# A decoder layer on one core: scores and projections two steps ahead until attention step 52 instead of 42

## The chip, the core and the metric

The kernel runs on one core of a Trainium2 chip. The metric is the time of one execution on the device in microseconds, as the median of several runs. The core has a matrix engine (TensorE, "PE" in the profile, with its weight loads as "PEld"), VectorE ("DVE"), ScalarE ("ACT"), GpSimd ("POOL") and SyncE ("SP"), which here only issues DMAs.

## What is computed

One decoder layer with pre-normalisation on x of shape 8 x 128 x 512, float32. Cut to what matters:

```python
# causal self-attention: 32 query heads, 8 key/value heads, head size 128
h = layernorm(x)
q, k, v = h @ w_q, h @ w_k, h @ w_v
probs = softmax(where(causal, q @ k.T * 128 ** -0.5, -inf))
x = x + (probs @ v) @ w_o
# attention over a context of the same shape
h = layernorm(x)
s = softmax(ctx @ h.T * 128 ** -0.5, axis=1)
x = x + s @ ctx
# gated feed-forward, three weight matrices packed in 4 bits
h = layernorm(x)
Wg, Wu, Wd = dequant(gate), dequant(up), dequant(down)
x = x + (silu(h @ Wg) * (h @ Wu)) @ Wd
```

The reference's attention over the context is `_L0_xattn_ref`, its 4-bit weights are those of `_L0_ffn_ref`.

## The kernel before

Every product is made from a high and a low 16-bit half of each operand, as three matmuls (high x high, high x low, low x high; `mm3`, lines 164 to 166). So each value that leaves the matrix engine is cast on ScalarE into its high half (line 118, in `split`) and subtracted on VectorE or GpSimd into its low half (line 121).

Self-attention is cut by key/value head into 8 groups `g` of four query heads, and by batch into two halves of four entries. A *unit* is one group with one half of the batch, a *step* is one group with one batch entry. There are 16 units of 4 steps, so 64 steps, numbered by `i`. The last four units are in another order than the rest: group 6 first half, group 7 first half, group 6 second half, group 7 second half (line 1050). Steps 40 to 43 are group 5 first half, 44 to 47 group 5 second half, 48 to 51 group 6 first half, 52 to 55 group 7 first half.

A step has four parts, each a function:

- `att_s` (line 587): the scores of one step, 12 matmuls into a bank of PSUM `ps_sc` (two banks, tag "s"); mask and row minimum on VectorE (line 608), exponentials on ScalarE (line 565), division by the sum on GpSimd (lines 575 and 622), the split into 16-bit halves `pb` on ScalarE and GpSimd, and a transposing DMA from `pb` to `pt`, issued on SP (line 636). The tile `s` has three buffers, `pb` two, `pt` three.
- `proj_piece` (line 1111, through `proj_parts`, line 1097): a quarter of the projections of one unit. Piece `j` of a unit makes one query head (`ps_q`, 12 matmuls of 512 columns); piece 0 also makes the unit's keys (`ps_k`), and pieces 1 and 2 of an even group make two batch entries of values each (`ps_v`), which are copied by two DMAs on SP (line 551). All of them share two banks of PSUM, tag "j". A piece's number is four times its unit plus `j`.
- `att_v` (line 639): probabilities times values, `ps_at`, five matmuls from line 645 on, then the cast `ah` (ScalarE) and the rest `al` (VectorE).
- `att_o` (line 653): those times the output weights, `ps_o`, 12 matmuls, added into `xr` on VectorE (line 662).

In `step(i)` the output product of step i-1 and the value product of step i come last, and before them the scores and the projection piece of a later step: one step ahead at the start, two steps ahead in the middle, one step ahead again afterwards. Two constants on line 1365, `SOON` and `BACK`, say when. At step `SOON` both the scores for one step and for two steps ahead are issued; at step `BACK` none, and neither a projection piece. From step `TAIL` = 53 on, `tail_step` (line 1335) takes over. It is one step ahead at first (scores two ahead from step 56 on) and mixes in the attention over the context. From step 53 on, the order on the matrix engine (until step 59) and on GpSimd is held to the order of the program. Elsewhere the order in which each engine gets its instructions is worked out when the kernel is built, from the program's order, the dependencies and estimated durations; it may pull later work forward where that is ready earlier. Once built, the order is fixed.

Between the steps other work is placed by step number. Weights of later groups are loaded into single buffers (`rawq`, `rawo`, `rawv`), their squares summed on ScalarE (`sumsq`, line 262, into `junk`) for a scale (lines 285 to 314), scaled on GpSimd (line 355) and split. The 4-bit weights of the feed-forward are unpacked on VectorE (lines 807 and 811) in steps 8 to 42. The context entries are loaded, summed and split in steps 43 to 53 (`c_load`, `c_prep`). The load of group 7's query weight is placed at step 40, and needs the buffer that group 6's last query weight leaves. The squares and the multiplies of this background work are held behind the exponentials and the multiplies of a given step, `pace["exp"]` and `pace["mul"]`; line 1400 picks that step.

Of the kernel before, what the change touches and what calls it, by code (L numbers as in the profile page):

```python
# [53 lines left out]
def tile_decoder(  # L54
# [1307 lines left out]
        for f in tail_x.pop((i, 1), ()):  # L1362
            f()

    SOON, BACK = 14, 42

    def step(i):
        g, b = steps[i]
# [118 lines left out]
```

## Time and profile before

| | us |
|---|---|
| median of three runs | 656.67 |
| lowest and highest of them | 656.52 to 656.84 |
| the profiled execution | 655.96 |
| its span, first to last instruction | 654.2 |

The granted clock of the matrix engine was 0.998 of full speed. The DMAs moved 69.34 MB, a mean of 106 GB/s. In the page's rows a group of instructions has a line of the kernel, an engine, an operation, what it writes and reads, a count, its busy time, the mean duration of one in nanoseconds, and the idle time of its engine before it with what ended most of that. These are the groups of the four parts of a step:

| part | group | count | mean ns |
|---|---|---|---|
| `att_s` | exponentials, ACT line 565 | 256 | 365 |
| `att_s` | mask and minimum, DVE line 608 | 256 | 310 |
| `att_s` | split of `pb`, ACT line 118 | 128 | 349 |
| `proj_piece` | cast `qh`, ACT line 118 | 64 | 571 |
| `proj_piece` | subtraction `ql`, DVE line 121 | 64 | 688 |
| `att_v` | cast `ah`, ACT line 118 | 64 | 582 |
| `att_v` | subtraction `al`, DVE line 121 | 64 | 683 |
| `att_o` | addition into `xr`, DVE line 662 | 64 | 747 |

Matmuls are pipelined: one of 512 columns is listed with some 378 ns but the next starts 216 ns after it. A stretch of the span can be asked for with the busy time of each engine in it; a timeline lists single instructions, with the idle time before one and what released it in square brackets.

### The profile page before, as it was taken

To read this page: it belongs to the slowest core of one execution; us is meant where nothing else is said; L and a number is where in the kernel's file an instruction comes from. 1 tells how busy PE (TensorE), PEld (TensorE's weight loads), DVE (VectorE), ACT (ScalarE), POOL (GpSimd) and SP (SyncE) were. 2 spreads that over 40 slices of the span, in tenths; PEclk is the share of its full clock that TensorE was granted. 3 is DMA by queue.
4 is the path that set the end of the run, shared out by engine and by line. 5 is a ranking of instruction groups with operands and counts; after the bars stand their busy time and mean duration, and the time that the engine had idled before them with its cause. 6 is when DMAs were issued, how large, how long until landed. Compare 5 with 4: busy or idle time off the path is not lost.

```text
span 654.2 us, 12431 instructions
## 1 busy us (share of the span) xinstructions
PE 629.8 (96%) x3992; PEld 342.3 (52%) x3992; DVE 465.6 (71%) x1475; ACT 439.3 (67%) x1238; POOL 380.8 (58%) x586
## 2 busy tenths in 40 slices
PE   8789999999999999999999999999999989999996
PEld 6455545565655555565555465556544434445443
DVE  6846676665767866576777555767776768988986
ACT  5687677465667675566667576866566478867674
POOL 7757477563747883475489395734577247612521
PEclk9999999999999999999999999999999999999999
DMA  9287254943763756355636414343544242102002
GB/s 316 48 171 170 75 72 122 229 105 79 190 164 88 187 137 160 95 168 127 151 94 167 143 41 122 66 92 74 89 67 68 39 93 50 31 19 65 1 1 64
DMA packets 117773, 69.34 MB, mean 106 GB/s; under 512 B 84190, under 2 KB 100593, under 8 KB 117708
## 3 DMA queue, kind: packets, MB, share of 16 engines
q1 hardware_dynamic: 117708, 68.55, 44.0%
q8 instruction: 31, 0.51, 0.3%
q14 instruction: 34, 0.28, 0.2%
HBM read 42.12 MB, written 2.20 MB: 68 GB/s over the span
## 4 chain that ended last, share of the span: by engine, by line
PE 73%; DVE 8%; DMA 6%; ACT 6%; POOL 4%; issue 2%; SPq 1%; DVEq 0%; ACTq 0%; POOLq 0%
PE ps_o L166 7%; PE ps_o L164 7%; PE ps_o L165 7%; PE ps_q L164 7%; PE ps_q L165 7%; PE ps_q L166 7%; PE ps_c L1181 6%; PE ps_c L1182 6%; DMA rawq<-in_L_attn_w_q_dram 3%; DMA pt<-pb 2%; PE ps_v L164 2%; PE ps_v L166 2%; PE ps_v L165 2%; PE ps_k L165 2%; PE ps_k L166 2%
## 5 line engine op out<-in xcount | busy, mean ns | idle before, releaser
L565 ACT ACTIVATE s<-s,negm 128x64 f32<-128x64 f32 (+1 forms) x256 | 93.1, 365 | 51.5 <-DVE negm L608 50.8
L164 PE MATMUL ps_q<-hT,wqh 128*128 128x512 f16 (+1 forms) x260 | 97.7, 376 | 1.6 <-DVE ql L121 1.6
L164 PE MATMUL ps_o<-woh,ah 128*128 128x512 f16 x256 | 97.0, 379 | 1.2 <-ACT ah L118 1.2
L166 PE MATMUL ps_o<-woh,al 128*128 128x512 f16 x256 | 96.9, 379 | 1.1 <-DVE al L121 1.1
L166 PE MATMUL ps_q<-hT,wql 128*128 128x512 f16 (+1 forms) x260 | 97.7, 376 | 0.0
L165 PE MATMUL ps_q<-hT,wqh 128*128 128x512 f16 (+1 forms) x260 | 97.7, 376 | 0.0
L165 PE MATMUL ps_o<-wol,ah 128*128 128x512 f16 x256 | 97.0, 379 | 0.0
L121 POOL TENSOR_TENSOR pb<-s,pb 128x256 f16<-128x256 f32 (+1 forms) x128 | 72.6, 582 | 16.2 <-ACT pb L118 14.3
L662 DVE SCALAR_TENSOR_TENSOR xr<-ps_o,unsc,xr 128x512 f32<-128x512 f32 x64 | 47.8, 747 | 41.3 <-PE ps_o L166 34.4
L575 POOL TENSOR_SCALAR rec<-rec 128x4 f32<-128x4 f32 x64 | 14.2, 222 | 108.1 <-DVE rec L573 87.5
L121 DVE TENSOR_TENSOR ql<-ps_q,qh 128x512 f16<-128x512 f32 x64 | 44.0, 688 | 40.3 <-ACT qh L118 40.2
L608 DVE CUSTOM_DVE_ANT_0 s<-ps_sc,mask,soft 128x64 f32<-128x64 f32 (+1 forms) x256 | 67.1, 310 | 4.0 <-PE ps_sc L166 1.9
L622 POOL TENSOR_TENSOR s<-s,rec 128x128 f32<-128x128 f32 (+1 forms) x128 | 63.6, 518 | 4.8
L118 ACT CAST pb<-s 128x256 f16<-128x256 f32 (+1 forms) x128 | 42.8, 349 | 28.1 <-POOL s L622 24.7
L118 ACT CAST ah<-ps_at 128x512 f16<-128x512 f32 x64 | 37.2, 582 | 21.9 <-PE ps_at L166 15.9
L565 ACT ACTIVATION_READ_ACCUMULATOR s<-s,negm 128x1 f32 x256 | 48.0, 188 | 0.0
L121 DVE TENSOR_TENSOR al<-ps_at,ah 128x512 f16<-128x512 f32 x64 | 43.7, 683 | 3.4 <-ACT ah L118 2.9
L1194 DVE TENSOR_SCALAR ps_c<-ps_c,rTg 128x512 f32<-128x512 f32 (+1 forms) x56 | 40.7, 750 | 7.0 <-PE ps_c L1182 6.4
L1192 ACT ACTIVATE ps_c<-ps_c,rTu 128x512 f32<-128x512 f32 (+1 forms) x57 | 36.2, 659 | 11.4 <-PE ps_c L1182 9.3
L118 ACT CAST qh<-ps_q 128x512 f16<-128x512 f32 x64 | 36.6, 571 | 10.6 <-PE ps_q L166 9.6
L166 PE MATMUL ps_sc<-k,ql 128*128 128x128 f16 (+1 forms) x256 | 42.6, 206 | 0.5 <-DVE ql L121 0.5
L165 PE MATMUL ps_sc<-k,qh 128*128 128x128 f16 (+1 forms) x256 | 41.5, 206 | 0.0
(244 smaller groups left out, 1698.3 us busy)
## 6 DMA issues: line engine op xcount, KB each, us to landing
rawq<-in_L_attn_w_q_dram SPq DMA_DIRECT2D x8, 1024.0 KB, 5.8
rawo<-in_L_attn_w_o_dram SPq DMA_DIRECT2D x8, 1024.0 KB, 6.1
zi<-zd SPq DMA_DIRECT2D x26, 256.0 KB, 4.1
vd<-v SPq DMA_DIRECT2D x64, 64.0 KB, 2.4
qr<-_L_ffn_down_qweight_dram SPq DMA_DIRECT2D x10, 256.0 KB, 5.8
xr<-in_x_dram SPq DMA_DIRECT2D x8, 256.0 KB, 8.2
rawk<-in_L_attn_w_k_dram SPq DMA_DIRECT2D x8, 256.0 KB, 5.7
rawv<-in_L_attn_w_v_dram SPq DMA_DIRECT2D x4, 512.0 KB
```

The costliest lines, as they stand in the source:

```text
L118: a = nc.scalar.copy(hi, src)
L121: b = (lo_eng or nc.vector).tensor_tensor(lo, src, hi, ALU.subtract)
L164: nc.tensor.matmul(ps, lh, rh, start=start and i == 0, stop=False)
L165: nc.tensor.matmul(ps, lh, rl, start=False, stop=False)
L166: nc.tensor.matmul(ps, ll, rh, start=False, stop=stop and i == n - 1)
L565: exp = nc.scalar.activation(v, v, AF.Exp, bias=negm[:, j : j + 1], scale=-1.0, accum_out=sums[:, j : j + 1],)
L608: nc.vector.tensor_tensor_reduce(view, flat(ps, cols[j]), masks[j // 2], soft_t[g][:, j % 2 : j % 2 + 1], BIG, ALU.add, ALU.min, negm,)
L622: mul = nc.gpsimd.tensor_tensor(v, v, rec[:, 2 * k : 2 * k + 2].unsqueeze(2).to_broadcast([P, 2, (k + 1) * HQ]), ALU.mult,)
L662: return nc.vector.scalar_tensor_tensor(xr[b], ps, unsc_t[g], xr[b], ALU.mult, ALU.add)
L1181: nc.tensor.matmul(ps, lh, rh, start=r == 0, stop=False, skip_group_check=r > 0)
L1182: nc.tensor.matmul(ps, lh, rl, start=False, stop=True, skip_group_check=r > 0)
L1194: nc.vector.tensor_scalar(ps, ps, sc, None, ALU.mult)
```

## The change

`BACK` goes from 42 to 52. Step 42 now issues the scores of step 44 and projection piece 48, and so on; steps 42 to 51 are two ahead, and step 52 is the one that issues neither. From step 53 on the program is the same. Line 1400 uses `BACK` as well, so that background work placed in steps 42 to 51 is held behind the exponentials and multiplies of step i+1 instead of step i.

```diff
-    SOON, BACK = 14, 42
+    SOON, BACK = 14, 52
 
     def step(i):
         g, b = steps[i]
```

## The prediction

> **What bounds the kernel now.** I read the page first, for the engine that sets the pace, then the table of stretches, for where that engine stops, then the timelines of the one stretch where the change starts. The page's first part:
>
> ```profile
> PE 629.8 (96%) x3992; PEld 342.3 (52%) x3992; DVE 465.6 (71%) x1475; ACT 439.3 (67%) x1238; POOL 380.8 (58%) x586
> ```
>
> TensorE (PE) is busy 96% of the 654.2 us. Its 512-column matmuls start 0.22 us apart wherever nothing waits (365.37, 365.59, 365.81 in the timeline), so in such stretches only less matmul work could help, and the change takes none away. What can be won or lost is idle time of PE. The stretches from attention step 41 to the end of attention show where that is (columns: stretch, its length, then busy time of PE, weight load, VectorE (DVE), ScalarE (ACT), GpSimd (POOL), granted clock, DMA):
>
> ```profile
> core 0: us, PE busy (x) PEld busy (x) DVE busy (x) ACT busy (x) POOL busy (x), PEclk, DMA share, GB/s
> 340.00:360.00 20.00, 20.00 (x137) 10.83 (x135) 16.34 (x54) 14.29 (x46) 18.29 (x27) 1.00 0.59 142
> 360.00:380.00 20.00, 17.69 (x122) 9.75 (x121) 11.22 (x46) 12.63 (x41) 9.31 (x16) 1.00 0.43 126
> 380.00:400.00 20.00, 20.00 (x130) 11.64 (x128) 9.45 (x31) 12.26 (x38) 18.48 (x27) 1.00 0.26 55
> 400.00:420.00 20.00, 20.00 (x139) 10.68 (x138) 15.04 (x77) 16.59 (x53) 10.40 (x18) 1.00 0.35 102
> 420.00:440.00 20.00, 20.00 (x131) 11.03 (x130) 12.74 (x54) 13.40 (x47) 9.91 (x16) 1.00 0.49 96
> 440.00:460.00 20.00, 20.00 (x159) 12.62 (x157) 14.73 (x58) 12.28 (x36) 9.71 (x18) 1.00 0.29 60
> 460.00:500.00 40.00, 37.52 (x266) 19.87 (x264) 28.03 (x112) 22.91 (x77) 26.80 (x44) 1.00 0.48 78
> ```
>
> Value products (line 645) of step 42 start at 361.03 and those of step 53 at 451.98. So the ten steps that the change re-orders, 42 to 51, lie in 360 to 440, and PE idles there in one place only: 20 - 17.69 = 2.31 us between 360 and 380, which is where the kernel drops from two steps ahead to one. The four waits of PE that make it up:
>
> ```profile
> 368.79 0.39 PE L164 MATMUL ps_o<-woh,ah 128*128 128x512 f16 x1 [0.57 <-ACT ah L118]
> 370.11 0.39 PE L166 MATMUL ps_o<-woh,al 128*128 128x512 f16 x1 [0.47 <-DVE al L121]
> ...
> 377.99 0.28 PE L645 MATMUL ps_at<-pt,vd 128*128 128x256 f16 x1 [0.63 <-DMA pt<-pb]
> 379.63 0.39 PE L164 MATMUL ps_o<-woh,ah 128*128 128x512 f16 x1 [0.64 <-ACT ah L118]
> ```
>
> The sum is 0.57 + 0.47 + 0.63 + 0.64 = 2.31. Counted by matmul starts against the usual spacing it is 2.97 (0.74 + 0.63 + 0.80 + 0.80), because the profile lets a matmul last longer than the next one waits. Two of the four wait for `ah`, the casts of attention results of steps 42 and 43. Why the first was late, from ACT's timeline:
>
> ```profile
> 360.63 0.40 ACT L118 CAST pb<-s 128x256 f16<-128x256 f32 x1 [0.27 <-POOL s L622]
> 365.60 0.63 ACT L262 ACTIVATE junk<-rawq 128x512 bf16<-128x512 f32 x1 [4.57 <-DMA rawq<-in_L_attn_w_q_dram]
> ...
> 368.17 0.56 ACT L118 CAST ah<-ps_at 128x512 f16<-128x512 f32 x1
> ...
> 369.25 0.34 ACT L565 ACTIVATE s<-s,negm 128x64 f32<-128x64 f32 x1
> ...
> 370.91 0.57 ACT L118 CAST k<-ps_k 128x512 f16<-128x512 f32 x1
> ```
>
> ACT stands 4.57 us on the sum of squares of the last query weight, whose load was issued at 359.74 and took 5.84 us. Behind it wait `ah` of step 42 (its matmuls were done at 363.90, it began at 368.17), the exponentials of step 44 and the evacuation of the key projection. The exponentials in turn hold up the probabilities `pt` of step 44, the third wait. VectorE stands behind the same load (3.5 us before its line 285).
>
> **The change part by part.** *The work moved.* Before, steps 43 to 52 issue scores for steps 44 to 53 and projection pieces 48 to 57; after, steps 42 to 51 do. No instruction is added or taken away. Moved one step up are 10 x 12 score matmuls (0.67 us a step, 452.55 to 453.22), 10 query pieces and 3 key pieces of 12 matmuls at 0.216 us (13 x 2.6 = 33.7 us) and 6 value pieces (12 x 0.109 = 1.3 us each, 7.8 us): 48 us of PE work, the same on both sides, so 0. The same for what hangs on it: 40 exponentials of 0.365 us, 40 masked reductions of 0.31, 10 + 3 casts of 0.57 with their subtractions of 0.69, 6 value evacuations, the POOL multiplies and splits.
>
> *Queues.* On SP go 10 probability transposes (1.2 us of queue each) and 12 value copies (0.6 each). A transpose of step i+2 now waits for its softmax one step earlier in the program, and context loads, weight loads and value copies queue behind it; SP already stands 29.5 us (12.6 + 11.9 + 3.1 + 1.9 in its waits by releaser) on such transposes between 380 and 460 with PE never idle there, so 0, and up to one `pt` wait (0.63 us) if that cover is gone. POOL and ACT meet the softmax ahead of `ah` instead of behind it. Priced at 0, because the same order has run in 340 to 360 at 20.00 of 20; without that cover one `ah` wait, 0.64 us.
>
> *Weights.* Projections move up by about one step, some 8 us, but their weights do not. The last group's four low parts are ready at 378.55, 379.66, 388.72 and 394.40 and its matmuls begin at 401.35, 407.59, 413.35 and 417.02: at least 22 us of slack, of which 8 go. 0. Value tiles (8 buffers) come free at least one step before they are needed, as in the earlier groups. 0. The pacing on line 1400 names the exponentials of one step later for steps 42 to 51; these too are issued a step earlier, so background work keeps its place. 0.
>
> *The gain at step 42.* Step 42 issued nothing but its output and value products; now scores of 44 and the key and query pieces of 48 come first. These 5.9 us had been pulled forward anyhow (they run from 359.07 to 368.1), so what is new as cover is the next step's: scores of 45 and query piece 49, 0.67 + 2.6 = 3.3 us, against 1.04 us of idle before 370.2; for the pair at 378 it is the softmax of step 44 that gets a place ahead of `ah`. Bounds: 0, if both projection banks are still full when PE gets there (the key cast at 370.91 frees one), and 2.31 to 2.97, if all four waits close. I take 2.31: moving the cast and the exponentials ahead of `ah` in the program is just what opens both banks.
>
> [...]
>
> *The step without scores and projections moves to 52,* right before the order written out by hand begins. There output products of step 51 follow the value products of 51 with little between them. Cover: value products of 52 (0.55 us) and, pulled forward, scores of 54 and query piece 58 (0.67 + 2.6), 3.8 us in all. Need: the shortest distance from value to output products in the trace is 2.1 us where PE did not idle (step 55: 468.38 to 470.47). Cost 0; 2.97 if a wait as at step 42 is met there, the nearest row.
>
> *Sum.* The profiled execution took 655.96 us, 1.8 of it outside the span. 654.2 - 2.31 + 0 = 651.9 of span, 653.65 with what is outside. The profiled execution lies 0.71 below the median of 656.67, so against the median: **654.4 us**.
>
> **The rivals.** *A, the hole is only moved, and grows (slower).* ACT's wait for the load stays ahead of everything, so 42 keeps its 2.97 us; at 52 the hand-written order lets PE pull nothing past a late `ah`, and a second 2.97 is paid. 656.67 + 2.97 = 659.6. For it: ACT also waits for context loads near there (2.24 us at 428.71). Against: PE idles 0 us from 380 to 460. It decides if `ah` of step 51 comes more than 3.8 us after its value products.
>
> *B, nothing to be seen.* The gap at 42 stays or moves whole, nothing else: 656.7. For it: scores and projections were pulled forward already, so the written order may matter little. Against: two banks then filled, which is what stopped PE.
>
> *C, the order of the rest shifts.* ACT and DVE are not held to the written order late in attention, and PE idles 2.48 us in 460 to 500 and 3.05 in 500 to 540. A shift by half of these 5.5 us each way: 653.9 or 659.4. For it: small waits of 0.3 to 1.1 us there hang on softmax and transposes. Against: from step 53 the issue order is the same in both kernels.
>
> **How the numbers follow.** What a measurement of this kernel tells from no change is about 0.2%, 1.3 us. Forecast (1.3 to 3.5 us saved): 0.44. A: 0.24. B: 0.19. C: 0.13, of it 0.03 on the fast and 0.10 on the slow side. Faster 0.44 + 0.03 = 0.47, same 0.19, slower 0.24 + 0.10 = 0.34. The forecast's own range is 653.2 to 655.4. The whole range reaches down to 652.6, where 2.97 and a little of C's gain fall together, and up to 660.0, past A by a small `ah` wait; about 0.2 is left outside.
>
> **What would show it.** Right: PE busy 20.0 of 20 in the stretch around the last query weight's load, exponentials of step 44 ahead of that weight's squares on ACT, and no new idle of PE between the value products of 51 and the output products of 52. Wrong: an `ah` wait of PE still at step 42, or one at 51 or 52 (A); idle of PE after 460 differing by more than 1.3 us (C). The forecast falls altogether if the wait for weights shows up as PE waiting on `wqh` or `wql`.

## The result, and the profile after

The changed kernel took 658.56 us (median of 22 runs, 656.68 to 660.38) against 656.47 for the kernel before, run beside it. The ratio is 1.0025, 95% interval 1.0015 to 1.0035. That is the ratio of the means and stands for some 1.6 us; the medians lie 2.1 us apart. So the kernel became slower, where 2.3 us faster was forecast. A second set of runs gave 1.0016 (1.0006 to 1.0026). The kernel before measured against itself gave 1.0001 (0.999 to 1.0011).

The execution profiled first took 657.65 us, its span 655.9. Its page again shows PE at 96%:

```profile
PE 631.5 (96%) x3992; PEld 343.2 (52%) x3992; DVE 468.6 (71%) x1475; ACT 440.4 (67%) x1238; POOL 380.2 (58%) x586
```

The same stretches as before the change (stretch, length, then busy time of PE, PEld, DVE, ACT, POOL, granted clock, DMA):

```profile
340.00:360.00 20.00, 20.00 (x137) 10.96 (x136) 15.89 (x54) 14.74 (x48) 18.12 (x27) 1.00 0.59 141
360.00:380.00 20.00, 17.72 (x120) 9.92 (x119) 11.33 (x40) 11.70 (x39) 7.45 (x15) 1.00 0.43 129
380.00:400.00 20.00, 20.00 (x138) 11.66 (x137) 11.99 (x47) 14.63 (x45) 19.34 (x28) 1.00 0.27 57
400.00:420.00 20.00, 19.69 (x132) 10.40 (x131) 11.22 (x55) 14.54 (x48) 8.55 (x17) 1.00 0.29 87
420.00:440.00 20.00, 20.00 (x129) 10.87 (x127) 14.95 (x62) 14.86 (x44) 14.34 (x22) 1.00 0.44 97
440.00:460.00 20.00, 19.43 (x137) 11.61 (x136) 14.45 (x59) 11.54 (x35) 6.96 (x14) 1.00 0.33 73
```

The idle time in 360 to 380 stayed (2.28 us instead of 2.31), and two new places joined it: 0.31 us in 400 to 420, 0.57 in 440 to 460. The rows of PE in its timeline that waited:

```profile
372.32 0.27 PE L164 MATMUL ps_v<-wvh,hT 128*128 128x256 f16 x1 [0.48 <-DVE ql L121]
...
374.35 0.17 PE L289 MATMUL ps_n<-sb,ones 128*128 128x4 bf16 x1 [0.89 <-DVE sb L285]
...
376.29 0.18 PE L289 MATMUL ps_n<-sb,ones 128*128 128x1 bf16 x1 [0.91 <-DVE al L121]
...
414.41 0.39 PE L164 MATMUL ps_o<-woh,ah 128*128 128x512 f16 x1 [0.21 <-ACT ah L118]
...
443.14 0.27 PE L645 MATMUL ps_at<-pt,vd 128*128 128x256 f16 x1 [0.57 <-DVE r L298]
```

All three places have the same thing in ACT's timeline, a sum of squares (line 262) that stands waiting for a load, with the cast `ah` of attention results behind it:

```profile
369.43 0.63 ACT L262 ACTIVATE junk<-rawq 128x512 bf16<-128x512 f32 x1 [3.06 <-DMA rawq<-in_L_attn_w_q_dram]
...
370.35 0.62 ACT L262 ACTIVATE junk<-rawq 128x512 bf16<-128x512 f32 x1
...
371.44 1.05 ACT L262 ACTIVATE junk<-rawo 128x1024 bf16<-128x1024 f32 x1
...
372.62 0.63 ACT L262 ACTIVATE junk<-rawq 128x512 bf16<-128x512 f32 x1
...
373.37 0.63 ACT L262 ACTIVATE junk<-rawq 128x512 bf16<-128x512 f32 x1
...
374.00 0.57 ACT L118 CAST ah<-ps_at 128x512 f16<-128x512 f32 x1
...
410.43 1.06 ACT L262 ACTIVATE junk<-rawo 128x1024 bf16<-128x1024 f32 x1 [2.30 <-DMA rawo<-in_L_attn_w_o_dram]
...
413.79 0.57 ACT L118 CAST ah<-ps_at 128x512 f16<-128x512 f32 x1
...
441.46 0.63 ACT L262 ACTIVATE junk<-c 128x512 bf16<-128x512 f32 x1 [1.22 <-DMA c<-in_ctx_dram]
442.09 0.57 ACT L118 CAST ah<-ps_at 128x512 f16<-128x512 f32 x1
```

They are group 7's query weights, its output weights and a context entry. (The sum over `rawo` at 371.44 is group 6's.) At the query weights the wait for the load is only the first part. When the load had landed, ACT worked for another 4.57 us (369.43 to 374.00) on what stood ahead of `ah`, all four query sums among it. Before the change only two of the four stood ahead, and `ah` began 2.57 us after the load (365.60 to 368.17).

To compare runs without the scatter of the start, I measure between marks: the first value-product matmul (line 645) of a step in the timeline. From step 40 to 53 lie the re-ordered steps; the idle time is PE's, summed over that stretch.

| kernel, profile | start to 40 | 40 to 53 | PE idle in it | 53 to 63 | 63 to the end |
|---|---|---|---|---|---|
| before, first | 349.70 | 102.28 | 2.31 | 77.75 | 124.46 |
| before, second | 351.49 | 102.30 | 2.15 | 77.74 | 124.48 |
| after, first | 350.38 | 103.29 | 3.16 | 77.74 | 124.47 |
| after, second | 350.61 | 104.15 | 4.03 | 77.73 | 124.48 |

The change acts in steps 40 to 53 alone, by +1.0 and +1.9 us. What follows is equal to a few hundredths, and what comes before scatters by 2 us whatever the kernel.

### The profile page after: what moved, and what is told of

Same layout as the page of the kernel before. It is cut to its first block, busy times and chain, and to the rows that moved or that the text cites. A ratio compares the mean times of both kernels' runs of the same rounds, so it can differ in the third digit from the quotient of the medians.

```text
span 655.9 us, 12430 instructions
## 1 busy us (share of the span) xinstructions
PE 631.5 (96%) x3992; PEld 343.2 (52%) x3992; DVE 468.6 (71%) x1475; ACT 440.4 (67%) x1238; POOL 380.2 (58%) x586
## 4 chain that ended last, share of the span: by engine, by line
PE 60%; POOL 12%; DVE 8%; DMA 7%; ACT 6%; issue 5%; SPq 1%; DVEq 0%; POOLq 0%; ACTq 0%
PE ps_c L1181 6%; PE ps_c L1182 6%; PE ps_o L166 6%; PE ps_o L164 6%; PE ps_o L165 6%; PE ps_q L166 5%; PE ps_q L164 5%; PE ps_q L165 5%; DMA pt<-pb 3%; POOL pb L121 2%; DMA rawq<-in_L_attn_w_q_dram 2%; POOL s L622 2%; POOL wql L121 2%; POOL wol L121 2%; DVE ps_c L1194 2%
## 5 line engine op out<-in xcount | busy, mean ns | idle before, releaser
L121 POOL TENSOR_TENSOR pb<-s,pb 128x256 f16<-128x256 f32 (+1 forms) x128 | 71.1, 571 | 19.8 <-ACT pb L118 18.0
L166 PE MATMUL ps_sc<-k,ql 128*128 128x64 f16 (+1 forms) x256 | 43.1, 207 | 0.5 <-DVE ql L121 0.5
```

What stands on the lines that cost most here:

```text
L121: b = (lo_eng or nc.vector).tensor_tensor(lo, src, hi, ALU.subtract)
L166: nc.tensor.matmul(ps, ll, rh, start=False, stop=stop and i == n - 1)
```

## The experiments

Theories: *P*, the pacing on line 1400 makes the load of group 7's query weights late; *O*, the new order of scores, projections and products costs by itself; later *L*, ACT meets the sums over late loads in front of the casts, whatever the order, and *H*, the step that issues no scores or projections leaves PE without cover. All ratios are to the kernel before, run beside it.

**Pacing and order apart.** Four kernels. Step 42's pacing undone in the changed kernel:

```diff
-paces[steps[i + (SOON < i < min(BACK, len(steps) - 1))]]
+paces[steps[i + (SOON < i < BACK and i != 42)]]
```

> The change with one thing undone: background work of step 42 alone is held behind the multiplies and exponentials of step 42, as before the change, not behind those of step 43. Theory P (pacing): in the changed kernel group 6's last query weight is finished 2.3 us later against the rest (362.70 instead of 359.35, of which 0.7 came in with the start), so group 7's load starts later and PE meets the wait for it. Then this kernel issues that load some 2 to 3 us earlier, PE idles less than 1.5 us in the 20 us around it instead of 2.28, and the time is 655.0 to 656.5, ratio to before 0.997 to 1.000. Theory O (order): scores and projections ahead of the output products cost by themselves. Then the time stays near 658, ratio 1.002 or more, with idle of PE after 400 as in the changed kernel (0.31 and 0.57 us).

The pacing of all ten steps undone:

```diff
-paces[steps[i + (SOON < i < min(BACK, len(steps) - 1))]]
+paces[steps[i + (SOON < i < 42)]]
```

> The change of order alone: pacing of steps 42 to 51 stays as before the change (background work behind step i, not i+1). Theory P: like the run with step 42 alone, ratio 0.997 to 1.000, because step 42 is the only step at which the pacing moves against the issue of the softmax by a whole step. Theory O: ratio 1.002 or more.

Pacing alone, with `BACK` at 42:

```diff
-paces[steps[i + (SOON < i < min(BACK, len(steps) - 1))]]
+paces[steps[i + (SOON < i < 52)]]
```

> The pacing alone: order of scores and projections as before the change, background work of steps 42 to 51 held behind step i+1. Theory P: the load of group 7's query weight starts later, the time goes up by 1 to 3 us, ratio 1.0015 to 1.005. Theory O: no change, ratio 0.999 to 1.001.

The pacing of step 42 alone, with `BACK` at 42:

```diff
-paces[steps[i + (SOON < i < min(BACK, len(steps) - 1))]]
+paces[steps[i + (SOON < i < 43)]]
```

> The pacing of step 42 alone, order as before the change. Theory P: as the run with the pacing alone, ratio 1.0015 to 1.005, since only this step holds the weight that the load waits for. Theory O: ratio 0.999 to 1.001.

| run | ratio (95%) | 40 to 53 | PE idle | query load issued after step 40's mark |
|---|---|---|---|---|
| step 42 paced as before | 1.0010 (0.9998 to 1.0022) | 103.76 | 3.75 | 9.66 |
| all paced as before | 1.0089 (1.0073 to 1.0104) | 109.02 | 5.74 | 9.71 |
| pacing alone | 0.9997 (0.9987 to 1.0007) | 103.03 | 2.60 | 12.37 |
| pacing of step 42 alone | 1.0039 (1.0022 to 1.0055) | 105.06 | 4.31 | 12.36 |

The load's issue obeys theory P exactly: about 9.7 us after the mark with step 42 paced as before (10.04 in the kernel before), 12.4 without (12.36 in the changed kernel). The times do not obey it: undoing all the pacing made the kernel much slower, and pacing alone changed nothing. Theory O had these two right (1.002 or more, and no change). But it too expected no change from the pacing of step 42 alone, which cost 2.6 us with the order untouched, and the first run, at 1.0010, lies outside the ranges of both. So these four runs decide for neither. The first shows why (stretches as above):

```profile
360.00:380.00 20.00, 19.57 (x136) 11.11 (x135) 11.32 (x45) 12.49 (x40) 8.34 (x16) 1.00 0.47 123
380.00:400.00 20.00, 19.31 (x126) 10.90 (x125) 10.06 (x39) 14.24 (x46) 19.06 (x28) 1.00 0.24 50
400.00:420.00 20.00, 17.99 (x125) 9.60 (x124) 11.28 (x58) 14.32 (x47) 7.62 (x16) 1.00 0.32 87
```

With the query load 2.7 us earlier, idle time around it falls to 0.43 + 0.69 = 1.12 us, as theory P had it, but at the output weights it grows from 0.31 to 2.01. Its ACT timeline there:

```profile
409.80 1.06 ACT L262 ACTIVATE junk<-rawo 128x1024 bf16<-128x1024 f32 x1 [4.00 <-DMA rawo<-in_L_attn_w_o_dram]
...
413.16 0.56 ACT L118 CAST ah<-ps_at 128x512 f16<-128x512 f32 x1
```

**The sums taken away.** In both kernels group 7 takes the scales of group 6:

```diff
-                at(m + 2, lambda g=g: (sumsq("q", g, 0, 0), sumsq("q", g, 0, 1)))
-                at(m + 3, lambda g=g: (sumsq("q", g, 0, 2), sumsq("q", g, 0, 3)))
-                at(m + 3, lambda g=g: (scales("q", g), scales("k", g), soft_scale(g)))
+                at(m + 3, lambda g=g: (sc_t.update({("q", g): sc_t["q", g - 1]}), scales("k", g), soft_scale(g)))
...
-            at(m + 1, lambda g=g: sumsq("o", g, 0, 0, 2))
-            at(m + 2, lambda g=g: sumsq("o", g, 1, 0, 2))
-            at(m + 3, lambda g=g: (scales("o", g), out_scale(g)))
+            at(m + 3, lambda g=g: (sc_t.update({("o", g): sc_t["o", g - 1]}), out_scale(g)))
```

> The changed kernel without the sums of squares and the scales of group 7's query and output weights (it takes those of group 6, so six activations, their small matmuls and their scale arithmetic are left out). Theory L (loads): PE's idle time between the value products of steps 40 and 53 is ACT and VectorE standing on group 7's two loads with the casts of attention results behind them. Then with nothing to sum ACT has no such wait, PE idles under 1.0 us in that stretch instead of 3.16, and the time falls by 2 to 3 us against the changed kernel, ratio to before 0.996 to 0.999. Theory O (order): the cost lies in the order of scores, projections and products itself. Then idle stays above 2.5 us and the ratio at 1.001 or more. A third place, the wait for a PSUM bank that the context's scale holds at step 52 (0.57 us), stays in both.

> The kernel before the change with the same sums and scales left out. Theory L: its 2.31 us of idle in the stretch go too, ratio 0.995 to 0.998, and it lies within 1 us of the changed kernel without the sums, since nothing is left that the two orders meet differently. Theory O: it is faster than the changed kernel without the sums by the same 1.6 us as with them.

Ratios 0.9944 (0.9929 to 0.9959) with `BACK` at 52 and 0.9958 (0.9944 to 0.9973) at 42. The first lies below the range expected by theory L. The stretch from 40 to 53 takes 99.06 and 99.05 us, with PE never idle in either. Three of the changed kernel's stretches without the sums:

```profile
360.00:380.00 20.00, 20.00 (x141) 11.52 (x139) 13.79 (x53) 10.13 (x35) 12.60 (x20) 1.00 0.49 133
...
400.00:420.00 20.00, 20.00 (x139) 10.99 (x138) 13.84 (x63) 13.94 (x45) 10.89 (x19) 1.00 0.45 110
...
440.00:460.00 20.00, 20.00 (x141) 11.60 (x139) 14.59 (x62) 11.78 (x40) 8.36 (x15) 1.00 0.35 59
```

So without those sums the order of scores, projections and products costs nothing and brings nothing in this stretch. The wait at step 52 went too, which I had not expected. These two kernels also have less work on ACT and VectorE; the complete kernels further down have all of it.

**The sums one step later** (changed kernel, `e = g == NG - 1` added to their steps):

> The changed kernel with group 7's sums of squares (query and output weights) placed one step later, nothing left out. Theory L: ACT's waits for the two loads (3.06 and 2.30 us) shrink or vanish, the waits of PE for attention results with them: idle of 1.0 to 2.5 us in the stretch, ratio 0.997 to 1.001. Theory O: ratio stays at 1.002 or more.

1.0056 (1.004 to 1.0072), idle 5.75 us. A miss: a step number does not fix where a sum lands in ACT's order. All four query sums still stood ahead of `ah` of step 42. At the query weights idle PE fell to 0.82 us (360 to 380), but everywhere behind them it grew: 1.42 us in 400 to 420, 2.07 in 420 to 440 and 1.44 in 440 to 460. ACT stood 3.90 us on the output weights and 3.04 and 3.20 on two context entries.

**The context's scale in another PSUM bank:**

```diff
-        ps = bank("a", [P, GH], "ps_n")
+        ps = bank("s" if kind == "c" else "a", [P, GH], "ps_n")
```

> The changed kernel with the small result of the context's scale in a bank of the scores instead of a bank of the value products. If the wait at step 52 (0.57 us, value products released by VectorE line 298) is for that bank, it goes, and PE idles 0.3 to 0.7 us less in the stretch between the value products of steps 40 and 53; the time falls by about as much (ratio 1.001 to 1.003), unless the scores now wait for their banks. If it was something else, the wait stays.

1.0028 (1.0011 to 1.0045). The wait of the value products went and the scores got it instead, 2.03 us in this profile, released by the same line 298. So it was for the bank, but the bank is only where the late sum reaches PE: ACT stood 2.80 us on that context entry. The ratio lies in the expected range, but idle PE rose from 3.16 to 4.60 us instead of falling.

**The sums held behind the casts.** Complete kernels again. `att_v` keeps the instruction of its `ah` cast in `pace["ah"]`, and group 7's sums may not be issued ahead of it; their scales come one step after them, and the preparation of the query weights comes one step later than before:

```diff
+    def behind(ins):
+        issue_after(ins, pace["ah"])
...
+                at(m + 4, lambda g=g: [behind(sumsq("q", g, 0, j)) for j in range(GH)])
+                at(m + 5, lambda g=g: (scales("q", g), soft_scale(g)))
...
-            at(c + j, lambda g=g, j=j: prep_wq(g, j))
+            at(c + j + (g == NG - 1), lambda g=g, j=j: prep_wq(g, j))
...
+            at(m + 3, lambda g=g: [behind(sumsq("o", g, i, 0, 2)) for i in range(2)])
+            at(m + 4, lambda g=g: (scales("o", g), out_scale(g)))
```

> The changed kernel, complete, with group 7's sums of squares held behind the cast of the attention results of steps 43 (query weights) and 47 (output weights), their scales one step later, and the preparation of the query weights from step 44 on. Theory L: ACT meets the loads with the data there, the casts are not behind them, PE idles under 1.0 us between the value products of steps 40 and 53, that stretch takes 99 to 100.5 us instead of 103.3, and the time is 653 to 655.5, ratio 0.995 to 0.999. If the waits come back elsewhere (VectorE's scale arithmetic, the small matmuls in PE's queue, late query weights), idle stays above 2 us and the ratio near 1.0.

> The kernel before the change with the same edit. Theory L: as the changed kernel with it, within 1 us of it, ratio 0.995 to 0.999, the stretch 99 to 100.5 us. If two steps ahead is worth something where the loads no longer stop ACT, the changed kernel with the edit is faster than this one by more than 1 us.

> The changed kernel once more, for a second profile. Theory L: idle of PE again at the two loads, 2.5 to 4 us in the stretch between the value products of steps 40 and 53, outside it no difference to before (77.7 and 124.5 us in the two stretches behind it). If the idle time is enough to lower the granted clock there, as in two of the runs, the stretch takes 2 to 3 us more than the 103.3 of the first profile. Ratio 1.0015 to 1.0035.

> The kernel before once more, for a second profile and to see how far two sets of runs of one kernel lie apart. Ratio 0.999 to 1.001, the stretch between the value products of steps 40 and 53 again 102 to 103 us, start to step 40 within 2 us of 349.7.

With `BACK` at 52 the ratio is 0.998 (0.9968 to 0.9991), the stretch 101.15 us with 1.69 idle; at 42 it is 0.9951 (0.9937 to 0.9965), 99.13 us and no idle. The repeated kernels are in the table of marks above. At both loads PE no longer waits. For the changed kernel the forecasts of idle (under 1.0 us) and of the stretch (99 to 100.5) were missed all the same, and the two kernels lie 2.0 us apart in the stretch (1.6 by their medians), not within 1. So with group 7's sums in place the order does still cost. What is left in the changed kernel is at steps 51 and 52; rows of ACT, DVE and PE there:

```profile
438.45 0.63 ACT L262 ACTIVATE junk<-c 128x512 bf16<-128x512 f32 x1 [1.70 <-DMA c<-in_ctx_dram]
439.08 0.57 ACT L118 CAST ah<-ps_at 128x512 f16<-128x512 f32 x1
...
439.20 0.16 DVE L285 CAST sb<-ssc 128x1 bf16<-128x1 f32 x1 [2.39 <-ACT junk L262]
...
440.14 0.27 PE L645 MATMUL ps_at<-pt,vd 128*128 128x256 f16 x1 [1.30 <-DVE r L298]
```

A context entry's sum, or the empty step (theory H)? The same hold on the context's sums tells:

```diff
-        at_x(XC + b + 1, lambda b=b: sumsq("c", b, 0, 0))
+        at_x(XC + b + 1, lambda b=b: issue_after(sumsq("c", b, 0, 0), pace["ah"]))
```

> The changed kernel, complete, with group 7's sums of squares held behind attention results and those of the context entries too, each behind the cast of its own step. Theory L: the waits at steps 51 and 52 (0.4 and 1.3 us of PE idle with group 7's sums alone held back) go, idle in the stretch between the value products of steps 40 and 53 is under 0.5 us, the stretch takes 99 to 99.7 us, ratio 0.994 to 0.997. Theory H (the step without scores and projections, now at 52, leaves PE without cover): idle of 1 us or more stays at steps 51 to 53, ratio 0.997 to 0.999.

> The kernel before with the same two edits. Both theories: no idle in the stretch, as with group 7's sums alone (99.1 us), ratio 0.994 to 0.997.

0.9953 (0.9941 to 0.9965) with `BACK` at 52 and 0.9945 (0.9933 to 0.9957) at 42; no idle in either, 99.14 and 99.20 us. The stretches of the first, with the empty step at 52 in place:

```profile
360.00:380.00 20.00, 20.00 (x143) 11.57 (x141) 13.89 (x46) 11.23 (x36) 11.17 (x18) 1.00 0.54 149
...
400.00:420.00 20.00, 20.00 (x138) 10.73 (x137) 13.18 (x60) 14.74 (x47) 10.06 (x18) 1.00 0.51 110
420.00:440.00 20.00, 20.00 (x144) 11.85 (x143) 14.41 (x62) 14.82 (x45) 14.76 (x23) 1.00 0.42 89
440.00:460.00 20.00, 20.00 (x143) 11.81 (x141) 15.09 (x62) 11.67 (x37) 6.99 (x13) 1.00 0.39 65
```

Theory H is refuted, and theory L holds at all three places. Three complete kernels are 3 to 4 us faster than the kernel before; where `BACK` stands no longer matters within their intervals. ACT still stands on loads there, for 1.49 us before 440.19 on a context entry in the changed kernel, but behind the cast `ah` of step 51, and PE does not idle. One thing stays open: the hold moves the sums behind the casts and the small matmuls of their scales to a later step, both at once, and no run separates the two.

## Why the prediction was wrong, point by point

- *What bounds.* Right. PE sets the pace (busy 96% of the span in both kernels), only its idle time moves, and before the change it lay in one place.
- *The gain at step 42.* Here the forecast failed. I took 2.31 us out of bounds that began at 0, with the argument that a cast and exponentials ahead of `ah` open both projection banks. They did run earlier: exponentials of step 44 began 13.1 us after step 40's mark instead of 19.6. But `ah` of step 42 still began 5.26 us after its value products were done (4.27 before), because the sums of squares, the thing that it waited for, stayed ahead of it, now all four over that load instead of two. And the scores and pieces that I counted as cover came ahead of those value products, which began 17.65 us after the mark instead of 11.33. PE then idled 2.28 us in other instructions: a projection bank (0.48), a small matmul of the scale that the sums feed (0.89), and a second one that VectorE's `al`, which needs `ah`, released (0.91). So 2.31 was forecast for this term and 0.03 us of idle went. I had read the late load as a fixed 4.57 us to be covered, and not asked which sum stands ahead of which cast in the new order.
- *Pacing, priced at 0.* Wrong in size, though not the cause by itself. For steps 43 to 51 background work keeps its place, as I said; at step 42 it does not, because the softmax of step 43 is issued at step 41 in both kernels. Group 6's last query weight moved behind that softmax, and the load that needs its buffer was issued 12.36 us after the mark instead of 10.04. The four runs on pacing show that no single sign follows from this: pacing alone gave 0.9997, at step 42 alone 1.0039.
- *Queues, priced at 0 because the same order ran in 340 to 360.* Wrong. That stretch held only one sum that met its load late (1.3 us); in 400 to 420 one for the output weights met its load 2.30 us late instead of 0.83, and PE idled 0.31 us (0.82 in the second profile). A stretch without such a sum ahead of a cast could not show what one costs.
- *The step moved to 52, cost 0.* Idle there was 0.57 and 0.72 us in the two profiles, but not for want of cover: with the context's sums held back the empty step costs nothing. What the term left out is ACT's wait on a context entry there, 1.22 us.
- *Weights.* Right: in the first changed profile PE waits nowhere in this stretch for `wqh` or `wql`.
- *Rivals.* A came nearest, by its sign and about half its price, and it named ACT's wait for context loads near 52; its mechanism, that the hand-written order keeps PE from passing a late `ah`, did not decide. C is out: what follows the mark of step 53 is equal to a few hundredths in all four profiles of the two kernels.

In all, 2.31 us of idle PE was to go; in the two pairs of profiles 0.85 and 1.88 us came instead (3.16 - 2.31 and 4.03 - 2.15).

## What to carry to other kernels

ScalarE stood 3.06 us here on a sum that waited for a load, and the cast `ah` behind it, whose value products were done at 368.74, began at 374.00; re-ordering the work around it only changed who was behind it. Look first for such instructions, and place them by an instruction that must go ahead, not by a step: one step later by number gave 1.0056, behind the casts 0.9953. When two orders are compared, take the suspected wait out of both; here that showed in one pair of runs that the order by itself was worth nothing. A gap in the bounding engine isn't a gain until what ends it has been followed to its first cause, in the new order as well as the old.

## What the hardware showed that was not expected

In two runs idle PE cost more than its idle time. In the run with all pacing undone PE waited 3.26 us in one piece for `ah`. The granted clock fell to half some 2.2 us into that wait (its mean was 0.66 in 410.5 to 411.0), and PE worked at half clock for about 6 us after it (the column before the last two is the granted clock):

```profile
400.00:408.00 8.00, 8.00 (x57) 4.29 (x56) 3.86 (x15) 3.77 (x14) 4.65 (x9) 1.00 0.79 174
408.00:411.70 3.70, 0.52 (x7) 0.21 (x3) 0.42 (x5) 2.33 (x6) 0.00 (x0) 0.86 0.12 20
411.70:418.00 6.30, 6.23 (x23) 2.56 (x24) 4.38 (x19) 5.90 (x20) 2.25 (x5) 0.54 0.16 42
418.00:424.00 6.00, 6.00 (x43) 3.23 (x42) 4.46 (x26) 4.74 (x15) 4.01 (x7) 1.00 0.18 36
```

At a clock of 0.54, 6.3 us hold the work of 3.4, so by this estimate some 2.9 us were lost on top. In the run with the context's scale in another bank the clock fell after three waits of 0.77, 0.90 and 0.91 us, with PE busy 2.92 of 5.5 us:

```profile
372.00:377.50 5.50, 2.92 (x23) 1.81 (x22) 4.39 (x16) 5.28 (x17) 0.12 (x2) 0.99 0.23 53
377.50:381.00 3.50, 3.50 (x11) 1.21 (x9) 1.87 (x10) 1.56 (x6) 2.36 (x6) 0.52 0.58 197
```

Its 512-column matmuls then start 0.43 us apart (378.13, 378.56, 378.98), and 0.22 apart before the waits. Gaps like these do not always do it. The changed kernel's two profiles, with waits of 0.48 or 0.68, 0.89 or 0.90, and 0.91 us in the same place, kept their full clock (1.00 in 360 to 380 in both); what decides it, no run shows, and whether some of the changed kernel's runs lost it, the times do not tell.
